# A four-stage block on one core: instructions that wait for a DMA held in program order, and one power for the two norms of a mixer

## The chip, the cores and the metric

The kernel runs on one core of a Trainium2 chip. A core has several engines, each with its own queue of instructions that it works off in order: TensorE (PE: matrix products and transposes), VectorE (DVE), ScalarE (ACT) and GpSimd (POOL, here element-wise work, masks and gathers by index). SyncE (SP) only issues transfers. Transfers themselves run on 16 DMA engines. An engine that waits for a semaphore holds up everything behind it in its own queue.

The metric is the device time of one launch in microseconds (us); lower is better.

## The reference

The input is x of 4 sequences, 512 tokens each, 256 channels. Four residual stages follow one another, each with a norm before and after:

```
x = x + layernorm(mixer0(layernorm(x)))     # state-space mixer with 32 heads, then a gated FFN
x = x + layernorm(experts0(layernorm(x)))   # 8 experts, the 2 best of each token
x = x + layernorm(mixer1(layernorm(x)))     # convolution, diagonal state-space scan, gate
x = x + layernorm(experts1(layernorm(x)))   # 8 experts, the 2 best, and one shared
```

mixer0 begins with a norm of its own, so that two norms follow directly on one another: `layernorm(x)` is `(x - mean) / sqrt(var + eps)`, and the first thing done with it is `h * rsqrt(mean(h*h) + eps)`. The mean square of h is `var / (var + eps)`.

```
h = rmsnorm(hidden_states, norm1_w)
h = mixer(h, in_proj_w, ...) + residual
residual = h
h = rmsnorm(h, norm2_w)
h = silu(h @ gate_w.T) * (h @ up_w.T) @ down_w.T
return residual + h
```

experts0 picks two of eight experts for every token: `relu(x @ w_fc[e])**2 @ w_proj[e]`, weighted with the softmax of the two router values. mixer1 computes, for each channel, `s[l] = a[l] * s[l-1] + u[l]` along the sequence, where a and u come from a step dt per head and token.

## The kernel before

The kernel is one Python function, `tile_layers`, which is traced once: each call of an engine's operation is recorded. A scheduler then arranges the recorded instructions for each engine's queue by estimates of its own, so an instruction may stand earlier or later in its queue than the trace had it. Two things set what is traced when.

**The main loop** (L826 to L905) goes over the sequences b = 0 to 3 and, in each, over 8 groups g of heads of mixer0. A group holds the input products and convolutions of its B and C (`load_pair`: products at L495, convolutions at L176 and L178, transposes at L646), the scores (`scores`: L655 the decay product, L658 its exponential on ACT, L663 the product of C and B, L666 their product on DVE, L669 the causal mask on POOL), the states (`states`, L679) and the outputs yA (L869) and yB (L874). Between these, `side.go(us, b)` traces steps of other work of sequence b - 1: its gated FFN (`feed_forward`, L280 and L294), and for b - 1 below 2 also the three parts of experts0. Each such part is a generator which yields triples: its time on TensorE, on DVE, and a time to let pass before its next step. The object `Side` takes the next step when those times have passed by its own count. `first(t)` (L567) and `second(t, k)` (L526) prepare a mixer: statistics, the two norms, the transposed input uT, the step dt (L593, copied at L596), its sums (L612), the decay tables Mv, and xcT (L545), zT and ebT (L555). For the first sequence they run at the start, interleaved with the first two `load_pair`s (L800 to L826); for the others from group 3 of the sequence before on. St and selE (L806 to L822) are constant tables built once from masks; 24 small transfers for each sequence and half (L533) then copy rows of Mv into St.

**The tail** (L1150 on) holds the FFN of the last sequence, experts0 of b = 2 and 3, mixer1 and experts1 of all four. A planner keeps a clock for TensorE and one for DVE, and goes from lane to lane (one lane for each stage), taking the next step of the best-ranked lane that is ready by the triples that it yielded.

**experts0** is in three parts. `experts0_in` (L303) routes the tokens and computes, for each of 15 tiles of 128 places, which token goes there (`token`) and which expert's weights belong to the tile (`wrow`). `experts0_out` (L391) fetches for each tile the token rows xr (128 KB, L401) and the weights wx (512 KB, L404) by indirect DMAs that POOL issues; step `three(t)` transposes xr of tile t+2 (L412, copied by ACT at L414), does the first product of tile t+1 (L419, relu at L422, square at L423) and the second of tile t-1 (L427), which ACT copies (L430) and sends to DRAM (L431). There are five buffers of xr and of wx; the FFN's weights share those of wx. `experts0_back` (L441) gathers for each token its two results (h and yg, L450), scales one on ACT (L454) and adds the other on DVE (L455).

**mixer1_out** (L1022) waits for a table dt by head that goes to DRAM as dD and comes back broadcast over partitions as db (L1029). Then, for each of four slices, POOL forms uu = db * X (L1033), ACT the exponential of db (L1034) and X * D (L1035), DVE the scan (L1038) and two operations behind it; TensorE does the output product (L1043).

**The norms.** `rsqrt` (L115) adds eps on DVE (L119) and raises to the power -0.5 on POOL (L121) with a tile `nhalf` of constants. In `first` it is called twice: r from the variance, then q = var * r * r and r2 = rsqrt(q) * r.

Of the kernel before, what the change touches and what calls it, by code (L numbers as in the profile page):

```python
# [8 lines left out]
F32 = mybir.dt.float32  # L9
# [28 lines left out]
def tile_layers(  # L38
# [28 lines left out]

    base = ctx.enter_context(tc.tile_pool(name="base", bufs=1))
# [30 lines left out]
    nhalf = base.tile([P, NC], F32, tag="nhalf", name="nhalf")  # L99
# [291 lines left out]
    def experts0_out(b, t, slack=1.2):  # L391
# [43 lines left out]
        yield 0.0, 0.0, 5.5  # L435
# [5 lines left out]
    def experts0_back(b, t, gap=1.0):  # L441

        y, rsb, (p1, p2) = YS[b % 2], h1s[b], t.p
        yield 0.0, 0.0, 3.0 + gap
        yg = wl.tile([P, NC, DM], F32, tag="v", name="yg", bufs=1)
        for c in range(NC + 2):
            if c < NC:
                for i in range(2):
                    j = i * NC + c
                    G.indirect_dma_start(out=(rsb, yg)[i][:, c, :], out_offset=None, in_=y,  # L450
                                         in_offset=bass.IndirectOffsetOnAxis(ap=t.place[:, j : j + 1], axis=0))
            if c > 1:
                r = rsb[:, c - 2, :]
                S.activation(r, r, AF.Copy, scale=p1[:, c - 2 : c - 1])  # L454
                V.scalar_tensor_tensor(r, yg[:, c - 2, :], p2[:, c - 2 : c - 1], r, ALU.mult, ALU.add)  # L455
            yield 0.0, 0.6, gap
# [14 lines left out]
    with ExitStack() as c1:  # L471
# [93 lines left out]
        def first(t):  # L565
# [231 lines left out]
        for b in range(1, B):  # L797
            nc.sync.dma_start(out=xs[b], in_=x_in[b].rearrange("(c p) d -> p c d", p=P))
# [8 lines left out]
        for k in range(2):  # L807
            z = w0.tile([P, 8, P], BF16, tag=f"St{k}", name=f"St{k}")
            V.tensor_tensor(z, pen.unsqueeze(1).to_broadcast([P, 8, P]),
                            named[:, k * 8 : k * 8 + 8].unsqueeze(2).to_broadcast([P, 8, P]), ALU.add)  # L810
            St.append(z)

        selE = w0.tile([P, 2, P], BF16, tag="selE", name="selE")
        for e in range(2):
            for k in range(2):
                V.tensor_copy(selE[:, k, :].rearrange("r (i e m p) -> r i e m p", e=2, m=4, p=8)[:, :, e],
                              named[:, k * 8 : k * 8 + 8].rearrange("r (i m) -> r i m", m=4)
                              .unsqueeze(3).to_broadcast([P, 2, 4, 8]))
# [12 lines left out]
        for b in range(B):  # L831
            ahead = batch(b + 1) if b + 1 < B else None
            aside = second(t, 1)
            for g, (k, m) in enumerate(order):
# [49 lines left out]
                side.go(3.0, b)  # L884
                if g >= 3 and ahead:
# [137 lines left out]
    def mixer1_out(b, t):  # L1023
# [247 lines left out]
```

## Time and profile before

| | us |
|---|---|
| three runs | 1321.13, 1323.87, 1330.15 |
| median | 1323.87 |
| the profiled execution | 1329.84 |
| its span | 1328.1 |
| TensorE busy in the span | 1153.0 |
| TensorE idle in the span | 175.1 |
| mean granted TensorE clock | 0.924 of full speed |

The profiled execution is 0.45% above the median. The busy times by stretch of the span, in us (the columns after the length: TensorE with the number of its instructions, its weight loads, DVE, ACT, POOL, then the granted clock, the share of the DMA engines and GB/s):

```profile
0.00:64.00 64.00, 35.18 (x91) 18.31 (x92) 39.79 (x106) 17.49 (x27) 21.03 (x96) 0.89 0.34 104
64.00:390.00 326.00, 297.86 (x1989) 173.88 (x1989) 203.44 (x350) 118.28 (x172) 52.96 (x63) 0.93 0.11 35
390.00:525.00 135.00, 121.53 (x864) 80.77 (x861) 74.72 (x130) 52.91 (x99) 44.06 (x46) 0.95 0.38 114
525.00:690.00 165.00, 154.90 (x984) 93.56 (x982) 108.16 (x192) 59.43 (x92) 25.05 (x31) 0.96 0.11 31
690.00:830.00 140.00, 127.53 (x909) 81.09 (x908) 81.78 (x152) 54.29 (x101) 50.99 (x51) 0.94 0.42 126
830.00:960.00 130.00, 119.92 (x617) 70.70 (x617) 70.42 (x183) 41.06 (x68) 25.79 (x26) 0.96 0.30 89
960.00:1130.00 170.00, 142.05 (x719) 107.01 (x718) 85.93 (x223) 84.02 (x173) 73.83 (x71) 0.90 0.47 142
1130.00:1328.00 198.00, 153.98 (x740) 94.18 (x738) 129.95 (x424) 116.05 (x250) 33.17 (x32) 0.86 0.09 29
```

The first stretch is the startup. 64 to 960 us is the main loop; the stretches from 390 to 525 and from 690 to 830 are those in which experts0 of b = 0 and of b = 1 run beside it. From 960 on it is the tail: first with experts0 of b = 2 and 3, from 1130 on mixer1 and experts1 alone. TensorE is idle in each stretch for what is left of its length: 28.8 us in the startup, 28.1 in the 326 us after it, 13.5, 10.1, 12.5, 10.1 in the next four, 28.0 and 44.0 in the tail.

### The profile page before, as it was taken

The numbers are of one execution on the slowest core, as the hardware profiler recorded it, in microseconds if no ns is written. First come the engines' busy times: TensorE is split into PE (matmuls) and PEld (weight loads), VectorE is DVE, ScalarE is ACT, GpSimd is POOL, SyncE is SP. The second block draws the span as 40 slices with busy tenths as digits, with TensorE's granted clock in tenths as the row PEclk, the third lists the DMA queues.
The fourth block names the chain that finished last, engine by engine and source line by source line (L and its number), as shares of the span: only waits on it lengthen the run. The fifth ranks groups of instructions, "written<-read, shape, count | busy, mean of one in ns | idle before, by whom it ended". The sixth has DMA issues, their size and how long they took to land.

```text
span 1328.1 us, 18538 instructions
## 1 busy us (share of the span) xinstructions
PE 1153.0 (87%) x6896; PEld 719.5 (54%) x6896; DVE 794.2 (60%) x1754; ACT 543.5 (41%) x980; POOL 326.9 (25%) x415
## 2 busy tenths in 40 slices
PE   4688988999889997899988998898998778888776
PEld 2354545455556663556655764554576666555543
DVE  5656565656755457656766465736437336576765
ACT  2343342333334334343323443324236355486644
POOL 5010201100243413210114423200333552220110
PEclk8899899999879998899989998998998888888878
DMA  5010001010132522101014533060435554110100
GB/s 183 19 34 24 26 18 33 18 52 17 48 116 82 171 89 75 33 17 53 17 34 143 162 113 112 1 179 16 151 103 156 176 153 139 42 40 9 41 16 24
DMA packets 76153, 97.41 MB, mean 73 GB/s; under 512 B 11008, under 2 KB 62208, under 8 KB 76064
## 3 DMA queue, kind: packets, MB, share of 16 engines
q0 software_dynamic: 13488, 45.10, 11.6%
q1 hardware_dynamic: 53936, 43.26, 10.8%
q10 hardware_dynamic: 8640, 7.87, 1.7%
q8 instruction: 55, 0.90, 0.3%
q14 instruction: 34, 0.28, 0.1%
HBM read 85.25 MB, written 12.12 MB: 73 GB/s over the span
## 4 chain that ended last, share of the span: by engine, by line
PE 64%; DVE 15%; POOL 6%; issue 5%; ACT 5%; DMA 4%; another core or an unknown queue 0%; SPq 0%; POOLq 0%; ACTq 0%; DVEq 0%
PE ps_pj L495 16%; PE ps_dc L280 6%; PE ps_dc L663 4%; PE ps_pj L679 3%; PE ps_dc L427 3%; PE ps_dc L294 3%; DVE BT L178 3%; PE ps_dc L419 3%; PE ps_yA L869 3%; PE ps_dc L940 2%; PE ps_b L1007 2%; PE ps_pj L646 2%; PE ps_yB L874 2%; DVE st L111 2%; DVE sc L666 2%
## 5 line engine op out<-in xcount | busy, mean ns | idle before, releaser
L495 PE MATMUL ps_pj<-uT,wg 128*128 128x512 f32 x512 | 268.5, 652 | 18.6 <-ACT sc L658 5.8
L178 DVE SCALAR_TENSOR_TENSOR BT<-ps_pj,col,BT 128x511 f32<-128x511 f32 (+2 forms) x192 | 143.1, 746 | 107.8 <-ACT BT L176 100.7
L669 POOL TENSOR_SCALAR_AFFINE_SELECT sc<-sc 128x1024 f32<-128x1024 f32 x64 | 70.2, 1096 | 434.2 <-DVE sc L666 406.5
L495 PEld LDWEIGHTS ps_pj<-uT,wg 128*128 128x128 f32 x512 | 94.3, 202 | 114.0 <-issue 81.9
L178 DVE SCALAR_TENSOR_TENSOR CT<-ps_pj,col,CT 128x511 f32<-128x511 f32 (+2 forms) x192 | 142.4, 742 | 20.8 <-ACT CT L176 11.7
L663 PE MATMUL ps_dc<-CT,BT 64*128 64x128 f32 x1024 | 95.6, 302 | 9.0 <-DVE sc L666 5.4
L663 PEld LDWEIGHTS ps_dc<-CT,BT 64*128 64x128 f32 x1024 | 75.1, 196 | 48.6 <-issue 34.2
L176 ACT ACTIVATE CT<-ps_pj,col 128x512 f32<-128x512 f32 x64 | 49.7, 777 | 122.4 <-PE ps_pj L495 117.2
L666 DVE TENSOR_TENSOR sc<-sc,ps_dc 128x1024 f32<-128x1024 f32 x64 | 77.7, 1215 | 30.3 <-PE ps_dc L663 20.2
L404 POOL DMA_INDIRECT wx<-in_w_exp_dram,wrow x60 | 61.2, 1020 | 112.5 <-PE ps_dc L427 70.2
L280 PE MATMUL ps_dc<-vT,wf 128*128 128x512 f32 x192 | 87.0, 595 | 0.3 <-ACT vT L137 0.3
L176 ACT ACTIVATE BT<-ps_pj,col 128x512 f32<-128x512 f32 x64 | 49.7, 777 | 90.9 <-PE ps_pj L495 87.8
L658 ACT ACTIVATE sc<-ps_dc 128x1024 f32<-128x1024 f32 x64 | 65.7, 1026 | 46.3 <-PE ps_dc L655 44.2
L427 PE MATMUL ps_dc<-wx,hx 128*128 128x256 f32 x240 | 69.8, 417 | 11.9 <-ACT hx L422 8.4
L419 PEld LDWEIGHTS ps_dc<-hx,wx 128*128 128x128 f32 x480 | 66.6, 204 | 20.4 <-issue 10.4
L419 PE MATMUL ps_dc<-hx,wx 128*128 128x128 f32 x480 | 70.2, 291 | 6.2 <-DMA wx<-in_w_exp_dram,wrow 4.3
L401 POOL DMA_INDIRECT xr<-XD,token x60 | 58.2, 971 | 69.2 <-PE ps_dc L412 53.8
L427 PEld LDWEIGHTS ps_dc<-wx,hx 128*128 128x128 f32 x240 | 46.1, 205 | 33.0 <-ACT hx L422 17.9
L423 DVE TENSOR_TENSOR hx<-hx 128x256 f32<-128x256 f32 x60 | 28.0, 466 | 54.0 <-ACT hx L422 48.1
L869 PE MATMUL ps_yA<-sc,xz 128*32 128x128 f32 x1024 | 52.2, 284 | 7.9 <-POOL sc L669 4.4
L280 PEld LDWEIGHTS ps_dc<-vT,wf 128*128 128x128 f32 x192 | 35.5, 190 | 41.0 <-issue 38.3
L679 PEld LDWEIGHTS ps_pj<-xd,bt 128*128 128x128 f32 x384 | 48.6, 200 | 12.9 <-issue 11.3
(311 smaller groups left out, 2014.5 us busy)
## 6 DMA issues: line engine op xcount, KB each, us to landing
wg<-in_w_in_dram SPq DMA_DIRECT2D x64, 256.0 KB
YS<-yr ACTq DMA_DIRECT2D x60, 128.0 KB
wf<-in_w_gate_dram SPq DMA_DIRECT2D x32, 128.0 KB
wf<-in_w_up_dram SPq DMA_DIRECT2D x32, 128.0 KB
wf<-in_w_down_dram SPq DMA_DIRECT2D x32, 128.0 KB
db<-dD SPq DMA_DIRECT2D x32, 128.0 KB
St<-Mv SPq DMA_DIRECT2D x192, 2.0 KB
x<-in_x_dram SPq DMA_DIRECT2D x4, 512.0 KB
```

The source lines that it names most:

```text
L176: S.activation(dst, p, AF.Identity, bias=bias, scale=w(3))
L178: V.scalar_tensor_tensor(dst[:, s:], p[:, : L - s], w(3 - s), dst[:, s:], ALU.mult, ALU.add)
L280: T.matmul(p, we[:, i * 2 + k, :], vT[:, k, :], start=(k == 0), stop=(k == 1))
L419: T.matmul(p[:, L + d * P : L + (d + 1) * P], w[:, k * DM + d * P : k * DM + (d + 1) * P], h[:, k * P : (k + 1) * P], start=(k == 0), stop ...
L427: T.matmul(p[:, 2 * P : 2 * P + DM], h[:, (2 + d) * P : (3 + d) * P], w[:, (2 + d) * DM : (3 + d) * DM], start=(d == 0), stop=(d == 1))
L495: T.matmul(p, w[:, k, :], uT[:, k, :], start=(k == 0), stop=(k == 1))
L658: S.activation(sc, df, AF.Exp)
L663: T.matmul(cb[:, e * L + c * P : e * L + (c + 1) * P], of.BT[e * 64 : (e + 1) * 64, c * P : (c + 1) * P], of.CT[e * 64 : (e + 1) * 64, c * ...
L666: V.tensor_tensor(sc, sc, cb, ALU.mult)
L669: G.affine_select(out=scv, in_=scv, compare_op=ALU.is_ge, fill=0.0, base=0, pattern=[[0, 2 * NC], [1, P]], channel_multiplier=-1)
L679: T.matmul(p[:, i * 48 : (i + 1) * 48].rearrange("p (e d c) -> p c e d", d=8, c=3)[:, c], pairs[i].bt[:, c, :], t.xd[k][:, c].rearrange("p ...
L869: T.matmul(yA[q * 32 : (q + 1) * 32, c * P : (c + 1) * P], xz[k][:, c, q, m, :], scs[q // 2][:, (q % 2) * L + c * P : (q % 2) * L + (c + 1 ...
```

## The change

`tc.keep_in_program_order` (called `later` in the kernel) takes an instruction just traced and adds an ordering edge to the instruction traced before it on the same engine: in its queue it can't stand ahead of that one any more. It adds no semaphore. It is put on

- both gathers of experts0_out (xr and wx, POOL) and TensorE's transposes of xr;
- the gathers of experts0_back (POOL), the scaling (ACT) and the sum (DVE) behind them;
- uu (POOL) and the exponential (ACT) of mixer1_out;
- the tables St and the copies to selE (DVE);
- the loads of x of sequences 1 to 3 (SP), which are no longer issued ahead of the first mixer but in group 1 of the sequence before.

The triples change at two places. experts0_out lets 2.0 pass after each of its three first fetches and 2.0 more, where it let 5.5 pass after all three. experts0_back lets 3 + 2 x gap pass before its first gather in place of 3 + gap, where gap is 4.0 for b below 2 and 1.0 in the tail.

In `first`, the two norms take one power: of var + eps for r, and of (1 + eps) var + eps^2 for r2, which is the same as the product that was formed before: rsqrt(var/(var + eps) + eps) / sqrt(var + eps). Three small DVE operations and one POOL power of 128x4 fall away in each of the four mixers, and the power that stays is of 128x8.

```diff
+    later = tc.keep_in_program_order
...
-    nhalf = base.tile([P, NC], F32, tag="nhalf", name="nhalf")
+    nhalf = base.tile([P, 2 * NC], F32, tag="nhalf", name="nhalf")
...
-                G.indirect_dma_start(out=xr[t], out_offset=None, in_=x,
-                                     in_offset=bass.IndirectOffsetOnAxis(ap=token[:, t : t + 1], axis=0))
+                later(G.indirect_dma_start(out=xr[t], out_offset=None, in_=x,
+                                           in_offset=bass.IndirectOffsetOnAxis(ap=token[:, t : t + 1], axis=0)))
...
-                G.indirect_dma_start(out=ws[t], out_offset=None, in_=w_exp,
-                                     in_offset=bass.IndirectOffsetOnAxis(ap=wrow[:, t : t + 1], axis=0))
+                later(G.indirect_dma_start(out=ws[t], out_offset=None, in_=w_exp,
+                                           in_offset=bass.IndirectOffsetOnAxis(ap=wrow[:, t : t + 1], axis=0)))
...
-                    T.transpose(p[:, k * P : (k + 1) * P], xr[t + 2][:, k * P : (k + 1) * P], ident)
+                    later(T.transpose(p[:, k * P : (k + 1) * P], xr[t + 2][:, k * P : (k + 1) * P], ident))
...
         for t in range(3):
             fetch(t)
-        yield 0.0, 0.0, 5.5
+            yield 0.0, 0.0, 2.0
+        yield 0.0, 0.0, 2.0
...
-        yield 0.0, 0.0, 3.0 + gap
+        yield 0.0, 0.0, 3.0 + 2.0 * gap
...
-                    G.indirect_dma_start(out=(rsb, yg)[i][:, c, :], out_offset=None, in_=y,
-                                         in_offset=bass.IndirectOffsetOnAxis(ap=t.place[:, j : j + 1], axis=0))
+                    later(G.indirect_dma_start(out=(rsb, yg)[i][:, c, :], out_offset=None, in_=y,
+                                               in_offset=bass.IndirectOffsetOnAxis(ap=t.place[:, j : j + 1], axis=0)))
...
-                S.activation(r, r, AF.Copy, scale=p1[:, c - 2 : c - 1])
-                V.scalar_tensor_tensor(r, yg[:, c - 2, :], p2[:, c - 2 : c - 1], r, ALU.mult, ALU.add)
+                later(S.activation(r, r, AF.Copy, scale=p1[:, c - 2 : c - 1]))
+                later(V.scalar_tensor_tensor(r, yg[:, c - 2, :], p2[:, c - 2 : c - 1], r, ALU.mult, ALU.add))
...
-            r = rsqrt(mv[:, :, 1], "rs")
-            q = small.tile([P, NC], F32, tag="q", name="q")
-            V.tensor_tensor(q, mv[:, :, 1], r, ALU.mult)
-            V.tensor_tensor(q, q, r, ALU.mult)
-            r2 = rsqrt(q, "rq")
-            V.tensor_tensor(r2, r2, r, ALU.mult)
+            ve = small.tile([P, 2, NC], F32, tag="rse2", name="ve")
+            V.tensor_scalar_add(ve[:, 0], mv[:, :, 1], EPS)
+            V.tensor_scalar(ve[:, 1], mv[:, :, 1], 1.0 + EPS, EPS * EPS, ALU.mult, ALU.add)
+            rr = small.tile([P, 2, NC], F32, tag="rs2", name="rr")
+            G.tensor_tensor(rr.rearrange("p a c -> p (a c)"), ve.rearrange("p a c -> p (a c)"), nhalf, ALU.pow)
+            r, r2 = rr[:, 0], rr[:, 1]
...
-        for b in range(1, B):
-            nc.sync.dma_start(out=xs[b], in_=x_in[b].rearrange("(c p) d -> p c d", p=P))
...
-            V.tensor_tensor(z, pen.unsqueeze(1).to_broadcast([P, 8, P]),
+            later(V.tensor_tensor(z, pen.unsqueeze(1).to_broadcast([P, 8, P]),
...
-                V.tensor_copy(selE[:, k, :].rearrange("r (i e m p) -> r i e m p", e=2, m=4, p=8)[:, :, e],
+                later(V.tensor_copy(selE[:, k, :].rearrange("r (i e m p) -> r i e m p", e=2, m=4, p=8)[:, :, e],
...
+                if g == 1 and ahead:
+                    later(nc.sync.dma_start(out=xs[b + 1], in_=x_in[b + 1].rearrange("(c p) d -> p c d", p=P)))
...
-            G.tensor_tensor(s, a[:, m, :], X[:, m, :], ALU.mult)
-            S.activation(a[:, m, :], a[:, m, :], AF.Exp, scale=An[:, m : m + 1])
+            later(G.tensor_tensor(s, a[:, m, :], X[:, m, :], ALU.mult))
+            later(S.activation(a[:, m, :], a[:, m, :], AF.Exp, scale=An[:, m : m + 1]))
```

More of the change, by code (lines that the diff above doesn't have):

```diff
@@ L808, in tile_layers @@
             z = w0.tile([P, 8, P], BF16, tag=f"St{k}", name=f"St{k}")
-            V.tensor_tensor(z, pen.unsqueeze(1).to_broadcast([P, 8, P]),
-                            named[:, k * 8 : k * 8 + 8].unsqueeze(2).to_broadcast([P, 8, P]), ALU.add)
+            later(V.tensor_tensor(z, pen.unsqueeze(1).to_broadcast([P, 8, P]),
+                            named[:, k * 8 : k * 8 + 8].unsqueeze(2).to_broadcast([P, 8, P]), ALU.add))
             St.append(z)
@@ L815, in tile_layers @@
             for k in range(2):
-                V.tensor_copy(selE[:, k, :].rearrange("r (i e m p) -> r i e m p", e=2, m=4, p=8)[:, :, e],
+                later(V.tensor_copy(selE[:, k, :].rearrange("r (i e m p) -> r i e m p", e=2, m=4, p=8)[:, :, e],
                               named[:, k * 8 : k * 8 + 8].rearrange("r (i m) -> r i m", m=4)
-                              .unsqueeze(3).to_broadcast([P, 2, 4, 8]))
+                              .unsqueeze(3).to_broadcast([P, 2, 4, 8])))
         for e in range(2):
```

## The prediction

> **What bounds the kernel now.** I read the table of engines first, then the chain that ended last, then the waits of TensorE, then the timeline where TensorE stands still, and last the busy times by stretch.
>
> ```profile
> span 1328.1 us, 18538 instructions
> PE 1153.0 (87%) x6896; PEld 719.5 (54%) x6896; DVE 794.2 (60%) x1754; ACT 543.5 (41%) x980; POOL 326.9 (25%) x415
> PE 64%; DVE 15%; POOL 6%; issue 5%; ACT 5%; DMA 4%; another core or an unknown queue 0%; SPq 0%; POOLq 0%; ACTq 0%; DVEq 0%
> ```
>
> TensorE is busy for 1153.0 of 1328.1 us, and the change leaves its 4622 instructions as they are. So all there is to gain is the 175.1 us in which it stands still, plus what the clock costs after a pause. The table of waits says what ended those pauses:
>
> ```profile
> PE ps_pj L646 <- DVE BT L178: 14.0, 13, 2.7
> PE ps_pj L133 <- POOL part L765: 13.7, 1, 13.7
> PE ps_dc L427 <- ACT hx L422: 8.4, 5, 5.8
> ...
> PE ps_pj L495 <- ACT sc L658: 5.8, 1, 5.8
> ...
> PE ps_dc L419 <- DMA wx<-in_w_exp_dram,wrow: 4.3, 1, 4.3
> ```
>
> The columns are total, times, longest. Three lines are one event each (13.7, 5.8 of the 8.4, and 5.8), and each lies where the change works: the startup, the last mixer, the combining of the experts. There is no line in which a transpose of gathered rows (L412) waits for xr: before, these gathers cost TensorE nothing.
>
> **The change part by part.** The profiled execution took 1329.84 us, its span is 1328.1, so 1.7 lie around it; it is 5.97 us (0.45%) above the median 1323.87. I sum against the span and take the difference off the median.
>
> *Startup.* The timeline:
>
> ```profile
> 6.85 0.17 DVE L119 TENSOR_SCALAR rse<-mv 128x4 f32<-128x4 f32 x1
> ...
> 7.18 1.03 POOL L121 TENSOR_TENSOR rs<-rse,nhalf 128x4 f32<-128x4 f32 x1 [5.38 <-DVE identb L98]
> ...
> 11.59 1.05 POOL L121 TENSOR_TENSOR rq<-rqe,nhalf 128x4 f32<-128x4 f32 x1
> ...
> 13.19 1.43 DVE L125 TENSOR_SCALAR u<-x,mv,rq 128x256 f32<-128x256 f32 x4
> ```
>
> The second power was ready at 9.52 (rqe, 9.27 + 0.25), stood behind memsets on POOL until 11.59, and the first product came 0.54 us after u, at 13.73. With one power: two small operations of 0.17 from 6.85, then the power from about 7.25. No 128x8 power is in the trace: at least the 1.03 of the 128x4, at most twice that; I take 1.1, since other small POOL rows hardly grow with so few columns. u starts near 8.35, the product at 8.9: 4.8 us sooner. Later mixers lose one of two powers and three small DVE operations each, beside other work: nothing.
>
> After that the change moves DVE work. In the trace St (L809, 19.66, 2.36 us, after a wait of 5.05 for POOL's named) and norms of x1 stand ahead of the copy of dt (23.49). Behind the pins, and with the loads of x1 to x3 issued inside the loop, neither can be there. dt follows its product (L593 at 15.99, 3.84 us, now near 11.2 to 15.0) at 15.1, 8.4 sooner; L612, 4.1 us later (27.58 before), starts near 19; the first CT near 21.3 instead of 29.78. But St (2.36) and the copies to selE (0.49) now stand before L545, and POOL's memset beside them adds 0.5: L545 moves from 45.24 to 38.3, and this is what is kept, **6.9 us**. The copies of St by DMA (24, begun at 39.01, 16.49 us) then begin near 37.3 and end near 53.8; the first L655 (64.73 before) would want them near 57.8. This is what is late next, with 4 us to spare. Of the SP queue: one x load stays ahead, the other two move behind weight loads; those have the whole first loop to land, nothing.
>
> *Combining of the experts (b = 0, 1).* The timeline at 494 us:
>
> ```profile
> 494.91 0.95 POOL L450 DMA_INDIRECT h<-YS,place  x1 [8.31 <-DMA YS<-yr]
> ...
> 497.42 0.95 POOL L450 DMA_INDIRECT h<-YS,place  x1 [0.30 <-issue]
> 498.26 0.51 ACT L454 ACTIVATE h<-h,p 128x256 f32<-128x256 f32 x1 [2.23 <-DMA h<-YS,place]
> ...
> 504.04 0.51 ACT L454 ACTIVATE h<-h,p 128x256 f32<-128x256 f32 x1 [2.35 <-DMA h<-YS,place]
> 505.11 1.01 ACT L658 ACTIVATE sc<-ps_dc 128x1024 f32<-128x1024 f32 x1
> ...
> 506.54 3.78 PE L495 MATMUL ps_pj<-uT,wg 128*128 128x512 f32 x4 [5.85 <-ACT sc L658]
> ```
>
> ACT waits in order for three gathers (2.2 to 2.4 us each), the exponential of the scores is queued behind them, TensorE stops for 5.85 us, and its next four products take 3.78 instead of 1.98 (the same row at 496.24). Sequence 1 shows 3.30 and 2.10 and again 3.78. Together 5.85 + 1.8 + 3.3 + 2.1 + 1.8 = 14.9. With the gap of the planner's steps raised from 4 to 8 us ahead of the first, and gather, scaling and sum held in trace order, the instruction order of the changed kernel puts mask operations (L669) between the gathers and the scaling two steps (8 us by the planner) behind its gather. From issue to use a gather takes 3.35 (494.91 to 498.26) to 4.1 us. I take 80%: **12 us**. The 20% is for h gathers that POOL now issues later, behind masks of 1.1 us.
>
> *Last mixer.* The row copy goes to DRAM and back (13.5 us from row to product). At 1104.6 ACT (5.31) and POOL (7.42) waited for db, hx of the experts was queued behind, and TensorE stopped for 5.78 with a product of 2.08 instead of 1.03: 6.8 us for b = 1. Holding uu and its exponential in trace order puts more between row and use there. For b = 0 the changed order has the exponential soon after the row, with hx behind it: up to 4.5 us, chance 0.6, 2.7. Net **4 us**.
>
> *What it costs.* The DVE work gone from the startup (St 2.36, selE 0.49, the norms of three x: 12 x 0.39 + 12 x 0.17 + small ones, about 10.7) is still done, now in steady stages where DVE runs at 62% (203.44 of 326.0 from 64 to 390): a third of it shows, **3 us**. ACT has four more table loads.
>
> *Table loads, row against rule.* Each takes 1283 ns in the trace and the next ACTIVATE follows at once (1104.60 + 1.28, then 1105.97, less than 0.1 later). The Trainium skill, "ScalarE: Activation LUTs", "What ACT_TABLE_LOAD costs", puts another 1380 ns of drain on each. By the row 5.1 us of ACT, by the rule 10.6. ACT is 41% busy; with 40% of it in TensorE's way that is 2 or 4 us. The row decides: **2 us**.
>
> *Gathered rows, row against rule.* 60 transposes are now held in trace order, as are the gathers, so their lead shrinks. By my count of product durations along the two instruction orders, for b = 0 and 1 the shortest lead of a transpose over its gather was 7.6 us before; now 6 of 30 have under 0.6 us left after a gather of 3.7, 4 more about 2. The rule of the skill, "DMA: Bandwidth & Descriptors", "Rules for kernel authors", speaks against this: issue a transfer early and wait for it late. By the rows (3.35 to 4.1) ten tiles wait some 0.3 us each on average: **3 us**. If the rule bites on all 60, since a 512 KB weight gather (wx) alternates with each xr on the queue and may delay it by an estimated 0.5 us, it is 30 us. The rows measured gathers of h beside yg, not behind wx, so this is the widest of the unknowns: 0 to 30.
>
> *POOL's queue.* Its masks (L669, 1.1 us) now stand behind pairs of fetches (1.25 us each, by the issue times 494.91, 496.17, 497.42) where before batches of four or five gathers could stand ahead of them. What waits behind a mask is yA (L869), 4.4 us in all before. It could lose these or as much again: I take nothing, since the number of gathers ahead of a mask falls for some and rises for others.
>
> Sum: -6.9 - 12 - 4 + 3 + 3 + 2 = -14.9. Span 1313.2, execution 1314.9, median 1323.87 - 14.9 = **1309**.
>
> **The rivals.** *A, the sum*: own range 1292 to 1318. *B, slower*: TensorE waits at L412 for xr. The scores, input products and states of the main loop are queued behind the transpose, so its wait is TensorE's. Gains of 22.9 less 5 of other costs leave 18 over 60 tiles: from 0.3 us a tile the gain is gone; at 0.55 us (33) it is +15, about 1339. For it: the lead is gone for ten tiles and a gather behind one of 512 KB was never timed. Against: POOL's masks no longer hold the gathers in batches, and wx, with an even larger transfer, made TensorE wait once in 60 (4.3). *C, only the startup holds*: the stalls of the combining move to another place (ACT waits at h whatever is pinned) and the last mixer gives back its 4: -6.9 and half of 8 in costs, near 1320, within 1%. *D, more*: the small ACT and DVE waits of the tail (L427, L1094, L1113, over 20 us together) shrink as well, near 1292. *E*, that the pins do nothing, is excluded by the instruction order, which differs on every engine.
>
> **How the numbers follow.** This kernel's measurement tells 1% (13 us, so 1310.6 and 1337.1) from no change. A 0.50, of which 0.34 lies below 1310.6 (some two thirds of its range) and 0.16 above it. B 0.28: 0.22 beyond 1337.1, 0.06 where the wait a tile is smaller, within 1%. C 0.10: 0.08 within 1%, 0.02 faster. D 0.12, faster. So faster 0.48, within 1% 0.30, slower 0.22. The range 1287 to 1342 holds A and C, D but for its far end (0.04) and B to a little over its middle (0.11 left out).
>
> **What would show it.** Right: the first L133 near 9 us and L545 near 38; no stop of over 3 us at L495 behind L454; the stop at L427 behind L1034 gone; TensorE's busy time within 5 us of 1153. Wrong: a line "L412 <- DMA xr" in the waits of TensorE of more than 10 us in total (B); L655 waiting for the copies of St; L1034 of b = 0 waiting for db with L427 behind it. The forecast falls if L412 waits more than 0.3 us a tile.

## The result, and the profile after

| | before | after |
|---|---|---|
| median of five runs each, us | 1327.11 (1321.13 to 1330.15) | 1366.56 (1361.33 to 1371.32) |
| ratio, 95% interval | | 1.0307 [1.0267, 1.0348] |
| the profiled execution, us | 1329.84 | 1361.33 |
| TensorE busy / idle in its span, us | 1153.0 / 175.1 | 1157.9 / 201.7 |

The changed kernel is 3.1% slower (three of the five runs of before are those of the table told earlier, whose median was 1323.87). In the profiled executions it is 31.5 us: 26.6 us more in which TensorE stands still, 4.9 us more in which it is busy. Line numbers of the changed kernel are 2 to 4 higher than those told so far (its L414 is the former L412, L1037 the former L1033 with uu, L1038 the exponential, L1044 the last operation before the output product, L1047 that product).

The head of its page:

```profile
span 1359.6 us, 18485 instructions
PE 1157.9 (85%) x6896; PEld 716.3 (53%) x6896; DVE 799.9 (59%) x1742; ACT 550.7 (41%) x984; POOL 324.6 (24%) x411
```

No engine has become the bound: the work is what it was. The chain that ended last can be followed back through only 5% of this span, so the table of TensorE's waits has to say where the time went (total, times, longest, in us):

```profile
PE ps_o L1047 <- DVE Gt L1044: 31.7, 10, 9.8
...
PE ps_dc L414 <- DMA xr<-XD,token: 10.1, 10, 3.0
...
PE ps_pj L135 <- DVE u L127: 9.6, 1, 9.6
...
PE ps_b L1003 <- DMA w1i<-in_w_in_dram: 8.1, 1, 8.1
...
PE ps_dc L429 <- ACT hx L424: 2.5, 6, 0.5
```

and of the same table of before, the row of the last mixer's output product:

```profile
PE ps_o L1043 <- DVE Gt L1040: 4.1, 3, 1.9
```

Two of the three single stops of before are gone (5.85 at the product behind the scaling of h, 5.78 behind db; L429 waits at most 0.5 now), and the third, in the startup, has shrunk from 13.7 to 9.6. Three new rows more than replace them. The output product of the last mixer (L1047) waits 31.7 us, where before it waited 4.1; the transposes of xr wait 10.1, where they had no row; the first input product of the last mixer waits 8.1 for its weight w1i, at the end of the main loop.

The longest row begins on POOL. The timeline of POOL alone, for the last mixer's b = 0:

```profile
995.15 1.26 POOL L1037 TENSOR_TENSOR uu<-db,X 128x512 f32<-128x512 f32 x1 [13.45 <-ACT hx L416]
1005.20 0.97 POOL L406 DMA_INDIRECT wx<-in_w_exp_dram,wrow  x1 [8.79 <-PE ps_dc L429]
...
1030.83 0.95 POOL L406 DMA_INDIRECT wx<-in_w_exp_dram,wrow  x1 [5.03 <-PE ps_dc L429]
...
1057.19 1.27 POOL L1037 TENSOR_TENSOR uu<-db,X 128x512 f32<-128x512 f32 x1
...
1075.53 1.27 POOL L1037 TENSOR_TENSOR uu<-db,X 128x512 f32<-128x512 f32 x1
...
1083.16 1.26 POOL L1037 TENSOR_TENSOR uu<-db,X 128x512 f32<-128x512 f32 x1
```

The four slices of uu start at 995, 1057, 1076 and 1083. Between the first and the second stand 25 gathers of rows and weights, and POOL stops in front of several of them until TensorE has released the buffer that the gather fills (8.79 and 5.03 us `<-PE ps_dc L429`). Between the second and the third stand the eight gathers of the combining of another sequence. Before the change the four slices started within 11 us, with two gathers between them:

```profile
1008.48 1.26 POOL L1033 TENSOR_TENSOR uu<-db,X 128x512 f32<-128x512 f32 x1 [1.99 <-DMA db<-dD]
1011.97 1.27 POOL L1033 TENSOR_TENSOR uu<-db,X 128x512 f32<-128x512 f32 x1 [2.23 <-DMA db<-dD]
...
1019.50 1.27 POOL L1033 TENSOR_TENSOR uu<-db,X 128x512 f32<-128x512 f32 x1 [1.66 <-issue]
```

What the hole in the changed kernel does to TensorE, in the timeline of all engines:

```profile
1076.83 0.72 ACT L1038 ACTIVATE db<-db,An 128x512 f32<-128x512 f32 x1 [2.82 <-POOL uu L1037]
...
1079.97 0.69 DVE L1044 SCALAR_TENSOR_TENSOR Gt<-Gt,uu 128x512 f32<-128x512 f32 x1
...
1080.72 3.78 PE L1047 MATMUL ps_o<-w1o,Gt 128*128 128x256 f32 x8 [9.78 <-DVE Gt L1044]
```

Each operation follows soon on the one before it. None of them is slow; the slice started late, and TensorE had 9.78 us with nothing to do. The eight products that follow take 3.78 us instead of the 1.99 that the eight of the next slice take at 1092.80.

That is b = 0, and 10.8 of the 31.7 us. Another 6.3 are b = 1's, where the fourth slice of uu (1157.01) stands behind a gather of the combining for which POOL waits 19.91 us (1154.74, `<-DMA YS<-yr`). In b = 2 and b = 3 (6.4 and 8.2 us) POOL has no gathers left. There uu stands behind powers of other stages' norms, which wait for DVE, and the pinned exponential behind other work of ACT and a table load. For b = 2:

```profile
1217.69 0.70 POOL L123 TENSOR_TENSOR rsf<-rsfe,nhalf 128x2 f32<-128x2 f32 x1 [19.11 <-DVE rsfe L121]
...
1218.36 2.49 POOL L1037 TENSOR_TENSOR uu<-db,X 128x512 f32<-128x512 f32 x2
...
1222.29 1.28 ACT L1038 ACT_TABLE_LOAD   x1
...
1223.59 0.72 ACT L1038 ACTIVATE db<-db,An 128x512 f32<-128x512 f32 x1
...
1228.23 3.20 PE L1047 MATMUL ps_o<-w1o,Gt 128*128 128x256 f32 x8 [4.07 <-DVE Gt L1044]
```

### The profile page after: what moved, and what is told of

Same layout as the page of the kernel before. It is cut to its first block, busy times and chain, and to the rows that moved or that the text cites. A ratio compares the mean times of both kernels' runs of the same rounds, so it can differ in the third digit from the quotient of the medians.

```text
span 1359.6 us, 18485 instructions
## 1 busy us (share of the span) xinstructions
PE 1157.9 (85%) x6896; PEld 716.3 (53%) x6896; DVE 799.9 (59%) x1742; ACT 550.7 (41%) x984; POOL 324.6 (24%) x411
## 5 line engine op out<-in xcount | busy, mean ns | idle before, releaser
L1047 PE MATMUL ps_o<-w1o,Gt 128*128 128x256 f32 x128 | 40.7, 472 | 31.7 <-DVE Gt L1044 31.7
L429 PE MATMUL ps_dc<-wx,hx 128*128 128x256 f32 x240 | 65.0, 395 | 3.2 <-ACT hx L424 2.5
L652 ACT COPY bt<-ps_pj 128x384 f32<-128x384 f32 x64 | 30.5, 477 | 70.7 <-PE ps_pj L650 70.0
L871 PE MATMUL ps_yA<-sc,xz 128*32 128x128 f32 x1024 | 48.2, 278 | 6.5 <-POOL sc L673 6.3
```

Of the source, the lines that this page charges most:

```text
L429: T.matmul(p[:, 2 * P : 2 * P + DM], h[:, (2 + d) * P : (3 + d) * P], w[:, (2 + d) * DM : (3 + d) * DM], start=(d == 0), stop=(d == 1))
```

## The experiments

There are eighteen runs, of fourteen kernels, in five series, each on one chip and beside runs of the kernel before on that chip. "Ratio" is to that kernel, with its 95% interval.

| label | what it is | series | ratio |
|---|---|---|---|
| c_after | the change whole, again | 2 | 1.0293 [1.0253, 1.0334] |
| e4_only_m1 | only the pins of the last mixer | 1 | 1.0094 [1.0069, 1.0119] |
| e1_no_m1 | all but these | 1 | 1.0274 [1.0189, 1.0358] |
| g1_no_m1_again | the same kernel | 3 | 1.0059 [1.0030, 1.0088] |
| e1b_no_exp | all, but of these only uu's | 3 | 1.0211 [1.0182, 1.0240] |
| e16_no_SV | all but the pins on scaling and sum | 2 | 1.0192 [1.0135, 1.0249] |
| e17_no_SV_m1 | and without those of the last mixer | 2 | 1.0024 [0.9997, 1.0052] |
| e2_no_fetch | all but the gathered rows' part | 1 | 1.0178 [1.0095, 1.0260] |
| e3_no_T | all but the pin on the transposes | 1 | 1.0379 [1.0297, 1.0461] |
| h2_fetch | only the gathered rows' part | 4 | 1.0242 [1.0203, 1.0282] |
| k3_fetch_again | the same kernel | 5 | 1.0171 [1.0124, 1.0217] |
| b3_back | only the combining's part | 2 | 0.9977 [0.9947, 1.0007] |
| k1_back_again | the same kernel | 5 | 0.9989 [0.9960, 1.0018] |
| f1_b3_pinw | with the first w1i product held | 3 | 1.0036 [1.0020, 1.0053] |
| h1_b3_w1i | with the load of w1i issued first | 4 | 1.0105 [1.0065, 1.0144] |
| k2_w1i_again | the same kernel | 5 | 0.9905 [0.9871, 0.9938] |
| b4_startup | only the startup's part | 3 | 1.0011 [0.9982, 1.0039] |
| k4_startup_back | startup and combining | 5 | 0.9970 [0.9942, 0.9997] |

In series 1 and 4 the profiles show waits put down to "remote", for which the instruction order gives no reason; the last section deals with them. A verdict below rests on series 2, 3 and 5, whose profiles have none of these of over 1 us, wherever one is to be had.

### The last mixer: uu and its exponential

```diff
-            later(G.tensor_tensor(s, a[:, m, :], X[:, m, :], ALU.mult))
-            later(S.activation(a[:, m, :], a[:, m, :], AF.Exp, scale=An[:, m : m + 1]))
+            G.tensor_tensor(s, a[:, m, :], X[:, m, :], ALU.mult)
+            S.activation(a[:, m, :], a[:, m, :], AF.Exp, scale=An[:, m : m + 1])
```

That is e1_no_m1 and g1_no_m1_again, against the changed kernel; e1b_no_exp takes only the second `later` away, and e4_only_m1 puts the two alone on the kernel before.

> The changed kernel with the two pins of mixer1_out (uu on POOL, its exponential on ACT) taken off, all else as changed. Theory M (these two pins are the loss: TensorE waits 31.7 us at the output product L1047 for Gt, against 4.1 before): the ratio to before falls from 1.031 to between 0.995 and 1.010, the waits at L1047 fall below 10 us in all, and ACT has fewer table loads. Theory F (the held gathers and transposes of rows are the loss): ratio stays above 1.020.

> The kernel before with only the two pins of mixer1_out added. Theory M: ratio 1.015 to 1.030, waits at the output product L1043 of 20 us or more. Theory F: ratio within 0.995 to 1.005.

> The changed kernel without the two pins of mixer1_out, as in the first run of this set, whose profile held 35.8 us of waits put down to another core or an unknown queue that no other profile has. Theory M (these pins cost about 27 us, as on the kernel without the pins on scaling and sum): ratio 1.006 to 1.016, L1047 waits 5 us in all. If it is near 1.027 again, the pins cost only where the pins of the combining are off as well.

> The changed kernel with the pin on the exponential (ACT) of mixer1_out taken off and the pin on uu (POOL) kept. If the exponential is what makes Gt late (it alternates with the gates of experts1 and loads a table each time): ratio near that of the kernel without both, 1.006 to 1.016. If uu is (it stands behind gathers on POOL): ratio stays at 1.024 or above.

The first pair seemed to say that both theories fail: the pins alone cost only 0.9%, and without them the change was still at 1.0274. But in e1_no_m1 the waits of L1047 had gone to 4.5 us, and what stood in their place were eight waits for "remote", 35.2 us together. On another chip (g1_no_m1_again) the same kernel has none of them and is 0.6% slower than before, where the whole change is 2.9 to 3.1% slower. TensorE's waits there:

```profile
PE ps_dc L414 <- DMA xr<-XD,token: 15.9, 11, 2.7
...
PE ps_b L1003 <- DMA w1i<-in_w_in_dram: 8.0, 1, 8.0
...
PE ps_o L1047 <- DVE Gt L1044: 4.5, 3, 2.8
```

and POOL's timeline at the same place, where all four slices are through before the next gather:

```profile
991.70 2.49 POOL L1037 TENSOR_TENSOR uu<-db,X 128x512 f32<-128x512 f32 x2 [15.99 <-DMA db<-dD]
997.21 2.06 POOL L1037 TENSOR_TENSOR uu<-db,X 128x512 f32<-128x512 f32 x1 [3.02 <-DVE Gt L1044]
1001.15 1.28 POOL L1037 TENSOR_TENSOR uu<-db,X 128x512 f32<-128x512 f32 x1 [1.88 <-DVE Gt L1044]
1006.20 1.07 POOL L406 DMA_INDIRECT wx<-in_w_exp_dram,wrow  x1 [3.78 <-PE ps_dc L429]
```

With uu's pin alone (e1b_no_exp, same series) L1047 waits 22.1 us and the first two slices start at 989.38 and 1051.24 with 25 gathers between them, so the 62 us hole is uu's. Within this series uu's pin is 1.0211 - 1.0059, about 1.5%. The exponential's is what is left to the whole change, 0.8 to 1.0% across series. By sequence, taking it off leaves b = 0 as it was (11.8 us) and halves the waits of the other three together (10.3 instead of 20.9). Table loads are the smaller part of it: the trace has 63 with both pins, 61 with uu's alone, 55 with neither.

Alone on the kernel before the pins cost less (1.0094; the product waits 23.7 us in e4_only_m1, and the first two slices stand 43 us apart, 1004.62 and 1047.20). The sizes do not add: the hole is as long as the row of gathers that stands in it, 17 there and 25 in e1b_no_exp. That the pins on the gathers are what keeps the other eight in it fits, but no run takes only these away.

### The combining of the experts

e16_no_SV takes two of its pins off the changed kernel, e17_no_SV_m1 those of the last mixer besides; b3_back (and k1_back_again) is the kernel before with the whole part:

```diff
-        yield 0.0, 0.0, 3.0 + gap
+        yield 0.0, 0.0, 3.0 + 2.0 * gap
...
-                    G.indirect_dma_start(out=(rsb, yg)[i][:, c, :], out_offset=None, in_=y,
-                                         in_offset=bass.IndirectOffsetOnAxis(ap=t.place[:, j : j + 1], axis=0))
+                    later(G.indirect_dma_start(out=(rsb, yg)[i][:, c, :], out_offset=None, in_=y,
+                                         in_offset=bass.IndirectOffsetOnAxis(ap=t.place[:, j : j + 1], axis=0)))
...
-                S.activation(r, r, AF.Copy, scale=p1[:, c - 2 : c - 1])
-                V.scalar_tensor_tensor(r, yg[:, c - 2, :], p2[:, c - 2 : c - 1], r, ALU.mult, ALU.add)
+                later(S.activation(r, r, AF.Copy, scale=p1[:, c - 2 : c - 1]))
+                later(V.scalar_tensor_tensor(r, yg[:, c - 2, :], p2[:, c - 2 : c - 1], r, ALU.mult, ALU.add))
```

> The changed kernel with the pins on the scaling (ACT) and the sum (DVE) of experts0_back taken off; the pins of its gathers and the longer gap stay. Theory T (held behind the end of the main loop, these two push the norm of the FFN of b = 2 past the last product L904, and TensorE meets w1i before it has landed; about 18 us between 865 and 937 us): ratio falls by 0.010 to 0.015 against the changed kernel on this chip, and no wait for w1i over 2 us. Rival (the loss is in the gathers that issue during the loop, or in mixer1_out alone): it stays within 0.004 of the changed kernel.

> As the kernel before this one, and the two pins of mixer1_out off too. Theory T with the pins of mixer1_out as the second loss (about 0.009, as they cost the kernel before): ratio within 0.995 to 1.010, waits at L1047 below 10 us. If the losses are not these two: above 1.015.

> The kernel before with only the pins of experts0_back (gathers, scaling, sum) and its longer gap. Theory T: slower by 0.008 to 0.016, with a wait of some 8 us of the first product with w1i; the stop of 5.85 us at L495 behind the scores of b = 0 is gone. My forecast of the combining, 12 us saved, would give 0.991.

> The kernel before with only the pins of experts0_back and its gap, again, to stand beside the next three on one chip. Where no profile of this chip shows waits put down to another core or an unknown queue: 0.995 to 1.001 as before. Where it does: slower by up to 0.013.

e16 and e17, in one series, measure the last mixer's pins a second time: 1.0192 - 1.0024, 1.7%, and L1047 goes from 32.1 to 5.0 us. With 1.0293 and 1.0307 less 1.0059 from the runs above, these pins are worth 1.7 to 2.5% beside the rest of the change, some 22 to 33 us.

Against c_after in the same series, taking the pins off scaling and sum wins 1.0% (e16_no_SV), as its theory T had it, and the wait for w1i is gone; but its four runs lie 18 us apart, and without the last mixer's pins the difference is 0.35% and across series (1.0059 and 1.0024). The same theory had the combining's part slower by itself, and b3_back is not.

b3_back shows the gain that was forecast, and its loss. The last output products of the main loop (L900), the first product with w1i and the transposes of h behind the loop (L133), first before, then in b3_back:

```profile
863.20 2.86 PE L900 MATMUL ps_pj<-wo,xcT 128*128 128x256 f32 x12 [0.89 <-POOL xcT L883]
...
900.95 1.88 PE L999 MATMUL ps_b<-xT,w1i 128*128 128x512 f32 x4
...
917.61 1.95 PE L133 MATMUL ps_dc<-ident,h 128*128 128x128 f32 x4 [5.74 <-ACT h L146]
```

```profile
851.38 5.38 PE L900 MATMUL ps_pj<-wo,xcT 128*128 128x256 f32 x12 [4.23 <-POOL xcT L883]
...
872.35 2.05 PE L999 MATMUL ps_b<-xT,w1i 128*128 128x512 f32 x2 [7.41 <-DMA w1i<-in_w_in_dram]
...
929.44 0.96 PE L133 MATMUL ps_dc<-ident,h 128*128 128x128 f32 x2 [7.25 <-ACT h L146]
```

The loop ends at 856.76 instead of 866.06. Of these 9.3 us about 4 are order (the kernel before has eight transposes of v and four FFN products behind it by then, b3_back has not), so about 5 are won. The transposes of h come 11.8 us later than before, of which about 2 are four more products with w1i already done. Between the two marks some 15 us are lost, and the wait for w1i is 7.4 of them. In the tail b3_back makes this up and ends 3.2 us ahead of before (spans of 1324.9 and 1328.1), but the gain is gone. Both the changed kernel and this one have there what the kernel before has not; the changed one's timeline, TensorE and the queue of SP:

```profile
864.35 0.55 SPq L922 DMA_DIRECT2D wf<-in_w_gate_dram  x1
...
868.28 0.45 SPq L965 DMA_DIRECT2D w1i<-in_w_in_dram  x1
...
880.52 2.04 PE L1003 MATMUL ps_b<-xT,w1i 128*128 128x512 f32 x2 [8.10 <-DMA w1i<-in_w_in_dram]
```

w1i is loaded from 868.28 on, behind six loads of FFN weights, and was used only some 12 us later. In the kernel before, w1i is loaded from 870.05 on, TensorE has FFN products to do in the meantime and reaches L999, the same product, at 900.95. With the pins the scheduler puts this product in front of the FFN's, and TensorE stands 8.1 us. e16_no_SV, which has neither pin on ACT and DVE, has no such wait.

Two kernels try to get this back from b3_back. f1_b3_pinw holds the first w1i product behind the work traced before it; h1_b3_w1i (and k2_w1i_again) leaves it where it is and issues its load ahead of the six:

```diff
-    last = last_feed_forward(B - 1)
-    next(last)
-
...
     w1i = weight(w1_in, "w1i")
+    last = last_feed_forward(B - 1)
+    next(last)
     w1g = weight(w1_gate, "w1g")
```

> The kernel before with the pins of experts0_back and its gap, and in addition the first input product of mixer1 of b = 0 held in trace order, so that it stands behind the FFN of b = 2. Theory T (the 14 us won in the loop are given back at its end, 7.4 of them at the product that waits for w1i): no wait for w1i, ratio 0.988 to 0.995 against 0.998 without it. Rival: the products only filled time in which TensorE had nothing else, and the ratio stays at 0.997 or goes up.

> The kernel before with the pins of experts0_back and its gap, and the load of w1i issued ahead of the six loads of FFN weights that stood before it. Theory T, second form (the loop's gain is lost because the first product with w1i waits 7.4 us for a load that is late, and the clock falls): the wait falls below 3 us, ratio 0.990 to 0.995. Rival (what is lost at the end of the loop is mostly other waits, for the norms of h and v, so that the wait for w1i only moves): 0.996 to 1.000.

> The same with the load of w1i first, again. If its 1.0105 came from the waits put down to an unknown queue (its instruction order up to the end of the main loop is that of the kernel above, which had 0.998 elsewhere), it is now within 0.003 of the kernel above; if it came from the earlier load, it is 0.010 slower than that again.

Holding the product takes the wait away and does not help (1.0036). The idle time comes back in pieces: 0.84 and 0.83 us in front of FFN products, 9.23 at the transposes of h where b3_back has 7.25, and 1.92 behind them; and the products with w1i, sixteen of which b3_back has done by then, are still to do. Loading earlier helps. In k2_w1i_again, TensorE and SP:

```profile
857.09 0.33 SPq L958 DMA_DIRECT2D w1i<-in_w_in_dram  x1
857.59 0.55 SPq L918 DMA_DIRECT2D wf<-in_w_gate_dram  x1
...
861.53 1.12 PE L998 MATMUL ps_b<-xT,w1i 128*128 128x512 f32 x2
```

The product follows its load by 4.4 us without a wait, the transposes of h start at 917.82 (k1_back_again: 927.83, in the same series), and the time is 0.9905 [0.9871, 0.9938], 1315.57 us against 1329.82. No other kernel here is faster than before by more than 0.3%. On the chip of series 4 the same kernel gave 1.0105, so the gain is not one for every run; what was different there is the subject of the last section.

### The gathered rows

```diff
             fetch(t)
-            yield 0.0, 0.0, 2.0
-        yield 0.0, 0.0, 2.0
+        yield 0.0, 0.0, 5.5
```

with `later` taken off both gathers and the transposes: e2_no_fetch, against the changed kernel. h2_fetch and k3_fetch_again put just these on the kernel before; e3_no_T takes only the pin on the transposes off the changed kernel.

> The changed kernel with the gathers xr and wx and the transposes of xr no longer pinned, and the single 5.5 in place of the four steps of 2.0; the pins of experts0_back, mixer1_out and the startup stay. Theory F: ratio falls to 1.005 or below, since the 10.1 us of L414 behind xr go and what is queued behind them. Theory M: ratio stays at 1.020 to 1.030; only the 10 us of L414 can go.

> The changed kernel with only TensorE's transposes of xr no longer pinned. Theory F: the 10.1 us of waits of L414 for xr go and the ratio falls by 0.008 or more, below 1.023. Theory M: it falls by less than 0.008, as the scheduler may put the transposes earlier, where they would wait for gathers that are still pinned.

> The kernel before with only the step of the fetches: gathers xr and wx and the transposes of xr held in trace order, and the four steps of 2.0. My forecast's step of 3 us: ratio 1.002. The slower rival of the forecast (every tile waits 0.5 us or more): 1.015 or above, waits of L412 for xr of 30 us. From the waits for xr in the changed kernel (10 to 16 us in 9 to 12 waits): 1.004 to 1.010.

> The kernel before with only the step of the fetches, again. Without waits put down to an unknown queue: 1.004 to 1.010, the 0.6% that the changed kernel keeps without the pins of mixer1_out. If it is 1.020 or above again, the fetches cost that by themselves, and the other parts win some of it back.

Alone, this part costs 1.7% where no "remote" waits disturb it (k3_fetch_again), and the longest row of TensorE's waits there is

```profile
PE ps_dc L412 <- DMA xr<-XD,token: 24.1, 12, 5.5
```

The kernel before has no such row. Yet TensorE stands still only 5.2 us longer than before in this profile (180.3 against 175.1), since other waits are shorter (that for hx at L427 falls from 8.4 to 2.8), and is busy 20.8 us longer (1173.8 against 1153.0): products behind a pause run slower, such as eight of L419 in 2.08 us behind a wait of 2.36 for xr, where others take 1.16. Not all of that is this part's either: the run is 3 to 8 us late before the experts run at all, with the same products in the same order (last section). Beside the rest of the change, this part is the difference between k4_startup_back (0.9970, xr 4.5 us in 2 waits) and g1_no_m1_again (1.0059, 15.9 in 11): 0.9%, some 12 us, though from two series.

e3_no_T went against the expectation that the transposes' pin is what shortens the lead. Without it the wait for xr doubles (21.1 us in 7, longest 9.6, against 10.1). That the scheduler, free again, brings transposes nearer to gathers that are still held is the likely reason, and was not followed up. In this profile the pin on the transposes limits the cost and does not make it. The run itself (1.0379) is one of series 1 with 10.4 us of "remote" waits, so its ratio is not read.

e2_no_fetch, at 1.0178, has 17.6 us of them and settles only this: L1047 still waits 15.6 us when no row gather of the experts is pinned. The loss there needs the pin on uu, not those on the gathers.

### The startup, and the sum of what is good

b4_startup is the kernel before with the one power, the pins on St and selE, and the loads of x moved into the loop; k4_startup_back has the combining's part too.

> The kernel before with only the startup's part: one power for both norms, the later loads of x, St and selE held in trace order. My forecast's step: 6.9 us saved less 3 for DVE's work put off, ratio 0.995 to 0.998. Rival (the gain is lost again by the third group, as the states at 116 us show in the changed kernel): 0.999 to 1.003.

> The changed kernel without the pins of the fetches and of mixer1_out: the startup's part and that of the combining alone. Sum of the single parts (1.0011 and 0.9977): 0.995 to 1.001. If the parts help each other, below 0.995 and better than both kernels.

> The changed kernel again, unedited, as the measure for the other three on this chip. Every theory: ratio to before near 1.031, as in its first runs. The three kernels of the first set that kept its main loop's instruction order were not steady in the main loop, so the waits there may differ from the first profile; the product L1003 waiting for w1i (8 us) and the waits at L1047 (about 30 us) should be there again.

The startup's gain does not last. In b4_startup the states' scan of the first sequence's groups starts 3.4 and 2.8 us sooner than before in the first two, and 0.5, 1.6 and 2.1 us later in the next three. Of the 3.3 us lost between the second and the third, 1.7 is one row of eight products (L495) that take 5.40 us where before they take 3.70, and the rest are waits for DVE's convolutions (2.40 for 1.60, 1.09 for 0.51). Such marks in one profile are good to a few us only (last section), so the verdict is the ratio: b4_startup ends at 1.0011, and its interval leaves no gain of over 0.2%. k4_startup_back at 0.9970 agrees with its two parts (1.0011 and 0.9977) taken together. c_after confirms the result on another chip.

## Why the prediction was wrong

The forecast was 1309, with 1287 to 1342 around it; the kernel takes 1366.56. All four signs that it set for being right came true (first products at 9.56, the one with selE at 37.42, no stop of over 3 us behind the scaling, the stop at the former L427 gone, TensorE busy within 5 us of 1153): they looked where the gains were. By its steps:

**Last mixer, forecast -4: this is the step that failed.** It measured +22 to +33 beside the rest of the change, and 0.9% alone. The text read the pins' effect at the first slice only: "Holding uu and its exponential in trace order puts more between row and use there", and for b = 0 it looked where the first exponential stands behind the row that it waits for. That reading was right (L429 behind hx waits at most 0.5 us, where it was 5.78). The other three slices were not followed through POOL's queue. In trace order the planner has put other lanes' steps between them. On POOL these are, for b = 0 and 1, gathers that wait until TensorE frees a buffer or rows have landed (17.1 of the 31.7 us at L1047), and for b = 2 and 3 powers of other stages' norms, with the exponential behind other work of ACT (14.6). Before the change the scheduler let uu pass them, and the row was 4.1 us. The prediction asked what stands behind a pinned instruction that waits, and not what a pinned instruction stands behind. No rival named it either; the waits for DVE's Gt would have been the row to ask about.

**Combining of the experts, forecast -12: the mechanism was right, the gain did not stay.** The stop of 5.85 us behind the scaling is gone, and b3_back leaves the loop 9.3 us earlier. But by the next landmark the gain is gone, and a wait of 7.4 to 8.1 us for w1i is new there. The step ended its account in the loop; what is late next (the load of w1i at its end) was not asked, and k2_w1i_again shows that the order of this load was worth about 11 us on its chip (0.9989 to 0.9905). Why the scheduler moves the w1i product ahead of the FFN with these pins is not settled.

**Startup, forecast -6.9: won at its landmark, not kept.** The first products start at 9.56 (forecast 8.9); the power of 128x8 takes 1.66 us, where 1.1 was assumed because other small rows hardly grow (memsets of 128x2 and 128x16 take 0.11 and 0.12). The powers of before do grow, 0.70 us for 128x2 and 1.02 for 128x4, and a line through these two gives 1.66 for 128x8:

```profile
7.24 1.66 POOL L579 TENSOR_TENSOR rr<-ve,nhalf 128x8 f32<-128x8 f32 x1 [5.45 <-DVE identb L100]
...
8.94 1.53 DVE L127 TENSOR_SCALAR u<-x,mv,rr 128x256 f32<-128x256 f32 x4 [1.72 <-POOL rr L579]
...
9.56 2.18 PE L135 MATMUL ps_pj<-ident,u 128*128 128x128 f32 x8 [9.56 <-DVE u L127]
```

The product with selE (the former L545) starts at 37.42 (forecast 38.3, before 45.24), so the landmark was met. The first decay product behind it starts at 62.97 instead of 64.73, and by the fourth group nothing is left (states at 133.53, before 133.39). A gain at a landmark was taken for a gain at the end. The DVE work put off (+3) is part of this: from 64 to 390 us DVE is busy 209.5 us instead of 203.4.

**Gathered rows, forecast +3: mis-sized.** It is some 12 us with the rest of the change and up to 23 alone. The bounds given were 0 to 30, and the row named as the mark, L412 waiting for xr by more than 10 us, came out at 10.1 in the changed kernel and at 24.1 with the part alone. The Trainium skill's rule that the prediction weighed ("DMA: Bandwidth & Descriptors", "Rules for kernel authors": issue early and wait late) put 30 where the rows of h beside yg put 3, and the truth lies between: alone nearer to the rule, with the rest nearer to the rows. xr lands in 4.1 us and wx in 4.9 (medians from issue), and in the changed kernel 10 of 60 tiles are late, by 1.0 us on average. The trace agrees with the rule, and shows that it bites on a part of the tiles. What the prediction put at nothing is that products behind such waits run slower.

**Table loads, forecast +2:** four more, 63 against 59, as told. That the last mixer's pins bring eight of them (55 without) and the combining's part takes four away (55 in b3_back) was not seen. TensorE's 4622 instructions of the text are 6896 in both profiles; nothing hangs on it.

Along one chain of kernels the parts can be summed, though over several series: startup and combining -4 us (k4_startup_back), with the gathered rows +12 more (g1_no_m1_again), with the last mixer's pins +31 to +33 more, together 39 to 41, against 39 us measured in the first runs and 38 in c_after. The forecast had -16, +3 and -4 for these. So the sign was lost by one step, off by 26 to 37 us; the gathered rows add 9 to the error, and two gains that were real at their own place and mostly gone by the end add 12. Rival B has the direction and about a third of the loss, but not its main cause.

## What to carry to other kernels

A pin in program order costs what the instruction then stands behind: before setting one, list what is traced ahead of it on that engine, gathers that wait for a buffer and small operations that wait for another stage alike, and follow every slice of a loop and every sequence, not the first. A stall taken away in one stage counts only where the next stage's data is already there; moving the following weight load ahead (k2) was what turned the combining's pins from nothing into 0.9%, on the chip where that was measured. Judge a start that comes sooner by the whole time, and look for signs of loss where nothing is meant to change.

## What the runs showed of the hardware

**Waits without a visible reason.** On the chips of series 1 and 4 an engine's next instruction came up to 10 us late while POOL issued gathers back to back. In h1_b3_w1i:

```profile
738.84 0.95 POOL L404 DMA_INDIRECT wx<-in_w_exp_dram,wrow  x1 [0.30 <-issue]
741.53 1.28 ACT L658 ACT_TABLE_LOAD   x1 [10.21 <-remote]
...
743.90 0.69 PE L412 MATMUL ps_dc<-ident,xr 128*128 128x128 f32 x2 [7.14 <-ACT sc L658]
```

ACT sits 10.21 us in front of a table load, and TensorE waits 7.14 for what follows; k2_w1i_again, the same kernel on another chip, has no such wait. In e1_no_m1 it is DVE, 6.7 us before a scan of 0.35, while POOL issues six gathers. Such waits of over 1 us come to 35.2 us in e1_no_m1, 22.2 in h1_b3_w1i, 17.6 in e2_no_fetch, 17.5 in h2_fetch, 10.4 in e3_no_T, 3.4 in e4_only_m1 and 4.2 in the first profile of the kernel before; there are none in any kernel of series 2, 3 and 5. One kernel has a ratio of 1.0274 with them and of 1.0059 without, another 1.0105 and 0.9905. Not all of that is waiting: in both, TensorE stands still longer by 17 and 11 us and is busy longer by 25 (1168.3 against 1143.0, 1172.1 against 1146.8), at a lower mean granted clock (0.915 against 0.936, 0.913 against 0.933). Whether the waits brought the clock down is not shown. That the instructions themselves are fetched by DMA (the profile lists 89 packets of kind "instruction" in the changed kernel) and queue behind the gathers would explain it; this was only argued. The Trainium skill ("Runtime: NRT & Kernel Launch", "Instruction fetch mechanics") holds that the cost of this fetch is mostly hidden; no run here tells whether these waits are such fetches.

**The same products in the same order drift.** k3_fetch_again leaves the first sequence as it was, yet the states' scan there comes 0.3 us later than before in the first group and 6.2 in the fourth; eight products of L495 between the two take 5.61 us where before they take 3.70. b3_back, k1_back_again and k2_w1i_again keep within 0.3 us of the distance that they have to before at the first scan up to 364 us. The changed kernel's second profile has the first scan 9.0 us ahead of before, its first profile 4.8. So a mark in one profile says little below several us.

**A power grows with its columns.** On POOL the 128x2 power takes 0.70 us in most rows, the 128x4 one 1.02, the 128x8 one 1.66.
